# Two layers with a 3x3 convolution and a pole-residue spectral layer: a new border between forward transform and mixing, and the exponentials' argument reduction done by halves

## The chip, the cores and the metric

The kernel runs on one core of a Trainium2 chip, in one launch. The metric is the device time of that core in microseconds (us); lower is better. A core has TensorE (PE, whose weight loads are listed as PEld), VectorE (DVE), ScalarE (ACT), GpSimd (POOL) and SyncE (SP, which here only issues DMAs). Each engine works through its own queue in order.

## The reference

All data are float32; `x` has 16 images (B) of 16 channels (C) and 256x256 points (N).

```python
x = x + conv3x3_circular(groupnorm(x))            # layer 0
x = x + spectral(groupnorm(x))                    # layer 1

def spectral(x):
    alpha  = fft2(x)
    A, Bm  = 1/(omega1 - pole1), 1/(omega2 - pole2)       # 4 poles each per channel pair
    S      = einsum('ikpq,oikp,xikq->oxik', residue, A, Bm)
    r1     = einsum('biox,oxik->bkox', alpha, S)          # mixes the channels at each frequency
    r2     = einsum(alpha, A, Bm, residue)                # 'bkpq'
    x1     = ifft2(r1).real
    E1, E2 = exp(pole1 * ty), exp(pole2 * tx)             # complex exponentials
    x2     = einsum(r2, E1, E2).real
    return x1 + x2 / Nx / Ny
```

## The kernel before, in words

P is 128, the number of partitions. The program has four stages one after the other:

1. **Convolution** (to about 565 us): layer 0, with tables for later stages made beside it.
2. **Forward transform** (to about 1194 us): 64 units, four per channel, each one channel and four images. A unit loads rows, folds them (DVE, POOL), transforms lines (PE into `ps_y`, ACT L793 out) and columns (PE into `ps_x` and `psd`, ACT L833 copies `q`, DVE L837 to L840 writes the spectrum `spec`). After the fourth unit of a channel, `project` multiplies `psd` by a table (DVE L865, tile `pr`) and adds it up (POOL L866, `proj`), and `spec` goes to DRAM as `aD`, on SP's queue, for the last channel on ACT's (L976).
3. **Mixing** (about 1219 to 1861 us): 32 groups `g` of four rows of frequencies, each in four steps `n`.
4. **Inverse transform** (to the end), which also takes in the exponentials from DRAM (`eD`).

In the mixing the order on every engine is the order in which the program is written (a hand order, without a scheduler). For each group there is:

- `weights(g)`: DVE L903 to L919, eight operations of 128x128, make the products `v` of A, and one POOL operation (L930) spreads them into `w`. For group 0 four ACT copies (L927) do that in the place of POOL. It is a generator, advanced one part at a time between other work. In the loop, weights of group g+2 are made in group g.
- `sums(n, w)`: 32 matmuls (L1032) that give a quarter of S for one group, into `ps_s`. `spread` copies them to the tile `sg` with ACT (L1049) and DVE stream shuffles (L1052). Group g+1's sums stand beside group g's mixing.
- `mix`: 64 matmuls per step (L1120) from `sg` and the loaded spectrum `abd` into four banks `ps_mix`, then four evictions to `yt` (L1233; three by ACT and one by DVE, or two and two when the step before has said `late`), then the store of `yt` to `yD` (SP, L1134) and the load of the next group's `abd` (SP, L1102 and L1107).
- one step of `exps`, a generator (`make_exps`) of the exponentials E1 and then E2, from group 1 on. It has 16 parts q (eight for each, two channels i per part) with seven steps each. Written as the engines see it: **first step** POOL makes the argument `th` (two of 128x256, L1180) and `rn`, the number of whole turns (L1181, L1183, L1184); **second** POOL subtracts `rn` times c1 and c2 from `th` (L1190 multiplies into `tmp`, L1191 subtracts); **third** the same with c3, two clamps (L1194, L1195), and ACT's two Exp of 128x256 into `ex` (L1198), which says `late`; fourth nothing; **fifth** ACT's Sin of `th` (L1201), `late` too; sixth POOL multiplies and folds into `ex` (L1203, L1205); seventh SP stores `ex` to `eD` (L1210; two stores per q for E1, one for E2). `th`, `rn`, `tmp` and `ex` have one buffer each; all but the two arguments of Exp are 128x512. In the profile `ex` is `s_ex`, `th` is `s_th`, `rn` is `s_rn`, `tmp` is `s_tmp`.

Frequencies come in pairs of a group and its mirror, so group 0 holds two halves: rows of group 0 proper (first 128 columns) and those of "group 32". **The border** before the loop is `first_sums`: POOL clears `pair` (`abd` 0 and 1, L1058), weights of 0 are finished and those of 32 made at once (L1059), the first `abd` loads are issued, `accs` is added on DVE (L1062), and then for both halves and four n the sums are made and copied: 128 columns to `sg` and two values to a small tile `other`, with group 1's weights made in between. DVE corrects two special columns with `other` (L1078, L1079), POOL clears `abd` 2 and 3 (L1081), and their loads follow. `finish_projections` (L1090 to L1092) turns `accs` with the table `jmat` into `o2`, for x2.

Memory: the tiles' pools are laid out by hand; a pool that reuses the place of another waits for that tile's last user.

Of the kernel before, what the change touches and what calls it, by code (L numbers as in the profile page):

```python
# [16 lines left out]
B = 16  # L17
# [7 lines left out]
def conv_then_laplace_kernel(ctx: ExitStack, tc: tile.TileContext, a: dict, out: bass.AP):  # L25
# [33 lines left out]
    cols = const("cols", [P, 24])  # L59
    kmask = const("kmask", [P, C])  # L60
    fold2 = const("fold2", [P, 2, 64])
    o2 = cp.tile([P, B, 2, 16], FP, name="o2", tag="o2")
    proj = cp.tile([P, 2, B, 16, 2], FP, name="proj", tag="proj")
    jmat = cp.tile([P, 3, P], FP, name="jmat", tag="jmat")

    def pitched(name, rows, row, *split):

# [87 lines left out]
    own = m16[:, 0:C:2]  # L155
    load_consts()
    halves[1] = [load_x(1, h) for h in range(2)]
    nc.sync.dma_start(out=jmat, in_=a["jmat"])
    ones = tp.tile([P, P], FP, name="ones", tag="ones")
    nc.vector.memset(ones, 1.0)  # L160
    tiny = wp.tile([P, 8], FP, name="tiny", tag="tiny")
# [567 lines left out]
    kpp = pool(p1, "sines", 3)  # L729
    prp = pool(p1, "prod", 2)  # L730
    bp = pool(p1, "b_const")
    u0 = pool(p1, "u0")
    pa = pool(p1, "p_y", 3, space=PSUM)
    px = pool(p1, "p_x", 4, space=PSUM)
    pd = pool(p1, "p_d", space=PSUM)
# [134 lines left out]
    units = [(i, b0) for i in range(C) for b0 in range(0, B, 4)]  # L870
    p2 = ExitStack()
    kp = pool(p2, "m_const", side="right")
    up = {"v": pool(p2, "v", side="right"), "u0": u0}

    p2k = kp.tile([P, 32, 2], FP, name="p2k", tag="p2k")
    nc.sync.dma_start(out=p2k, in_=a["pole2_k"])
# [18 lines left out]
    def weights(g):  # L895

        shape = [P, 32, 4]
        u = up["u" if g else "u0"].tile([P, 4, 32, 4], FP, name="u", tag="u")  # L900
        w, den, e, f = (u[:, j] for j in range(4))
        pr2, pre, pim = (prU[:, j].unsqueeze(2).to_broadcast(shape) for j in range(3))
        nc.vector.tensor_tensor(  # L903
            w,
            omg[:, g].unsqueeze(1).to_broadcast(shape),
            pims.unsqueeze(2).to_broadcast(shape),
            ALU.subtract,
        )
        nc.vector.tensor_tensor(den, w, w, ALU.mult)
        nc.vector.tensor_tensor(den, den, pr2, ALU.add)  # L910
        yield
        nc.vector.reciprocal(den, den)

        nc.vector.scalar_tensor_tensor(e, w, m1, pre, ALU.mult, ALU.add)
        nc.vector.scalar_tensor_tensor(f, w, nm0, pim, ALU.mult, ALU.add)
        yield
        v = up["v"].tile([P, 32, 2, 4], FP, name="v", tag="v")
        nc.vector.tensor_tensor(v[:, :, 0], e, den, ALU.mult)
        nc.vector.tensor_tensor(v[:, :, 1], f, den, ALU.mult)  # L919
        if g == 0:  # L920
            yield
        wt = wp.tile([P, 4, 8, 32], FP, name="w", tag="w")
        v2 = v.rearrange("p a r s -> p a (r s)")
        w4 = wt.rearrange("p a k (i m) -> p (a k) i m", i=4)
        if g == 0:
            for i in range(4):
                nc.scalar.activation(w4[:, :, i], v2, AF.Copy, scale=m4[:, i : i + 1])  # L927
            return wt
        full = [P, 32, 4, 8]
        nc.gpsimd.tensor_tensor(  # L930
            w4,
            v2.unsqueeze(2).to_broadcast(full),
            m4.unsqueeze(1).unsqueeze(3).to_broadcast(full),
            ALU.mult,
        )
        return wt
# [3 lines left out]
    nc.vector.memset(sgn[:, 0:1], -1.0)  # L940
    nc.vector.memset(sgn[:, 1:2], 1.0)
    rest = v_stats(B - 4, B, lambda: pa.tile([P, 512], FP, name="ps_y", tag="ps_y"))
    last, first_weights = None, weights(0)
    for u in range(len(units) + 1):
        at = units[u] if u < len(units) else None
        if at is not None:
            now = vq
            t = lp.tile([P, 2, 4, 3, P], FP, name="t", tag="t")
            if u + 1 < len(units):
                vq = fold(*units[u + 1], loaded.pop(u + 1))  # L950
                if u + 3 < len(units):
                    loaded[u + 3] = load_v(*units[u + 3])
                if u < 2:
                    next(rest)
            for j in range(2):
                lines(*at, now, t, j)
        if last is not None:
            i, b0 = last[:2]
            if b0 == 0:
                spec = (a0, a1)[i % 2].tile([P, 2, N, B], FP, name="spec", tag="spec")  # L960
                psd = pd.tile([P, B, 32], FP, name="psd", tag="psd")
            done = columns(*last, spec, psd)
        if at is not None:
            for j in range(2, 4):
                lines(*at, now, t, j)
                if u < 2:
                    next(rest, None)
        if u == len(units) - 4:
            first_constants()
        if len(units) - 4 < u < len(units):  # L970
            next(first_weights)
        if last is not None:
            first_slots(b0, spec, *done)
            if b0 == B - 4:
                project(i, psd)
                (nc.sync if i + 1 < C else nc.scalar).dma_start(  # L976
                    out=aD[:, 2 * i : 2 * i + 2], in_=spec.rearrange("p r f b -> p r (f b)")
                )
        last = (*at, t) if at is not None else None
    p1.close()  # L980
    ptab.close()
# [14 lines left out]
    pm = pool(p2, "p_mix", 4, space=PSUM)  # L996

    def new_sg(g):
        return (g0, g1)[g % 2].tile([P, N, 2 * C], FP, name="sg", tag="sg")

# [4 lines left out]
        z.tile([P, 4, 4, 16, B], FP, name=f"abd{j}", tag=f"abd{j}") for j, z in ((2, a1), (3, a2))  # L1005
    ]

    zp.tile([P, 384], FP, name="between", tag="between")
    ct = tp.tile([P, 4, 8, N], FP, name="ct", tag="ct")
    nc.sync.dma_start(out=ct, in_=cD)  # L1010
    def next_step(steps, w):
# [10 lines left out]
            except StopIteration as e:  # L1022
                return e.value

    def sums(n, w):

        ps = [pg.tile([P, 2, N], FP, name="ps_s", tag="ps_s") for _ in range(2)]
        for q in range(2):
            for iq in range(4):
                for odd in range(2):  # L1030
                    rows = slice(64 * odd, 64 * odd + 64)
                    nc.tensor.matmul(  # L1032
                        ps[odd][32 * iq : 32 * iq + 32, q],
                        lhsT=w[rows, iq, 2 * n + q],
                        rhs=ct[rows, iq, 2 * n + q],
                        start=True,
                        stop=True,
                    )
        return ps
# [14 lines left out]
    def first_sums():  # L1054
# [1 line left out]


        nc.gpsimd.memset(pair, 0.0)  # L1058
        wt, w128 = at_once(first_weights), at_once(weights(32))  # L1059
        load(0, 1)  # L1060
        steps, w1 = weights(1), None
        nc.vector.tensor_tensor(accs, proj[:, :, :, :, 0], proj[:, :, :, :, 1], ALU.add)  # L1062
        sg = new_sg(0)
        other = up["u"].tile([P, 2, 2 * C], FP, name="other", tag="other")
        for h, w in enumerate((wt, w128)):
            for n in range(4):
                fy = slice(P * h, P * h + P)
                ps = sums(n, w)
                spread(
                    n,  # L1070
                    (sg[:, fy], [z[:, :, fy].rearrange("p q n -> p n q") for z in ps]),
                    (other[:, 1 - h], [z[:, :, P * (1 - h)] for z in ps]),
                )
                if 4 * h + n in (3, 4, 5):
                    w1 = next_step(steps, w1)
        for h in range(2):
            o, d = sg[:, P * h], other[:, h]
            nc.vector.tensor_tensor(d, d, o, ALU.subtract)  # L1078
# [1 line left out]
        for jq in range(2, 4):  # L1080
            nc.gpsimd.memset(abd[jq], 0.0)  # L1081
            load(0, jq)
        return sg, w1

    def finish_projections():


        for ro in range(2):
            ps = pm.tile([P, B, 16], FP, name="ps_o", tag="ps_mix")
            nc.tensor.matmul(ps, lhsT=jmat[:, 0], rhs=accs[:, ro], start=True, stop=False)  # L1090
            nc.tensor.matmul(ps, lhsT=jmat[:, 2 - ro], rhs=accs[:, 1 - ro], start=False, stop=True)
            nc.vector.tensor_copy(o2[:, :, ro], ps)  # L1092

    def load(g, jq, rows=range(4)):

# [65 lines left out]
    def make_exps(which):  # L1161
# [10 lines left out]
        nc.gpsimd.tensor_scalar(pim, pl[:, :, 1], sign, None, ALU.mult)  # L1172
        for q in range(8):
            th = ep.tile([P, 2, N], FP, name="s_th", tag="s_th")
            rn = ep.tile([P, 2, N], FP, name="s_rn", tag="s_rn")
            tmp = ep.tile([P, 2, N], FP, name="s_tmp", tag="s_tmp")
            ex = ep.tile([P, 2, N], FP, name="s_ex", tag="s_ex")
            for j in range(2):
                i = 2 * q + j
                nc.gpsimd.tensor_scalar(th[:, j], t, pim[:, i : i + 1], None, ALU.mult)  # L1180
            nc.gpsimd.tensor_scalar(rn, th, 1.0 / (2 * PI), turns, ALU.mult, ALU.add)  # L1181
            magic = 1.5 * 2.0**23
            nc.gpsimd.tensor_scalar(rn, rn, magic, None, ALU.add)  # L1183
            nc.gpsimd.tensor_scalar(rn, rn, magic, None, ALU.subtract)  # L1184
            yield
            c1 = 6.28125
            c2 = float(np.float32(1.93500518798828125e-3))
            c3 = 2 * np.pi - c1 - c2
            for c in (c1, c2, c3):
                nc.gpsimd.tensor_scalar(tmp, rn, float(c), None, ALU.mult)  # L1190
                nc.gpsimd.tensor_tensor(th, th, tmp, ALU.subtract)  # L1191
                if c == c2:
                    yield
# [21 lines left out]

    p2.enter_context(tc.manual_schedule())
    accs = yp.tile([P, 2, B, 16], FP, name="accs", tag="yt")
    ahead, wt = first_sums()
    finish_projections()
    unmix = None  # L1220
    exps, late = chain(make_exps(0), make_exps(1)), None
    for g in range(32):
# [1 line left out]
        steps = weights(g + 2) if g < 30 else iter(())  # L1224
        ahead = new_sg(g + 1) if g < 31 else None
        for n in range(4):
            evict = sums(n, w_now) if ahead is not None else []
            yt = yp.tile([P, 2, 4 * B, 16], FP, name="yt", tag="yt")
            if evict:
                spread(n, (ahead, [z.rearrange("p q n -> p n q") for z in evict]))  # L1230
            for m in range(4):
                o, src = mix(4 * n + m, sg, yt)
                (nc.vector.tensor_copy if m >= (2 if late else 3) else nc.scalar.copy)(o, src)  # L1233
# [376 lines left out]
```

## Time and profile before

| what | us |
|---|---|
| median of three runs | 2618.05 (2610.47 to 2623.62) |
| profiled execution | 2623.94 |
| its span | 2622.1, mean granted TensorE clock 0.986 |
| mixing, 1219 to 1861 | 642, PE busy 602.5, DVE 504.9, ACT 406.9, POOL 389.2 |

A timeline row gives the start and the length in us, the engine, the line and operation, the tiles written and read, the shapes, how many there were, and in square brackets how long the engine had been idle before and what ended that. A row may stand for several instructions one after the other ("x64"); matmuls are pipelined and their lengths overlap. A row of a group gives the count, then busy us and mean ns, then the idle time ahead. A row of one line gives least, median and largest ns of one. A granted clock of 0.50 means that PE ran at half speed.

### The profile page before, as it was taken

To read this page: it belongs to the slowest core of one execution; us is meant where nothing else is said; L and a number is where in the kernel's file an instruction comes from. 1 tells how busy PE (TensorE), PEld (TensorE's weight loads), DVE (VectorE), ACT (ScalarE), POOL (GpSimd) and SP (SyncE) were. 2 spreads that over 40 slices of the span, in tenths; PEclk is the share of its full clock that TensorE was granted. 3 is DMA by queue.
4 is the path that set the end of the run, shared out by engine and by line. 5 is a ranking of instruction groups with operands and counts; after the bars stand their busy time and mean duration, and the time that the engine had idled before them with its cause. 6 is when DMAs were issued, how large, how long until landed. Compare 5 with 4: busy or idle time off the path is not lost.

```text
span 2622.1 us, 84262 instructions
## 1 busy us (share of the span) xinstructions
PE 2468.6 (94%) x35314; PEld 1885.3 (72%) x35314; DVE 1980.8 (76%) x3772; ACT 1432.6 (55%) x2599; POOL 1290.5 (49%) x1179
## 2 busy tenths in 40 slices
PE   5998999989999999998999999999799999999998
PEld 2444455567777777775878778788688888888887
DVE  7777788848888888887877878887276676667666
ACT  2565566666666666665666656666244444444443
POOL 1333378433333333333666645766555565555553
PEclk9999999989999999999999999999899999999999
DMA  7888878854655655655777777777988888888884
GB/s 274 276 279 282 294 270 294 297 211 177 240 195 209 242 220 194 245 225 190 225 229 214 226 225 222 222 227 228 253 302 289 291 292 279 299 289 287 291 287 174
DMA packets 318011, 653.17 MB, mean 249 GB/s; under 512 B 49174, under 2 KB 163990, under 8 KB 305728
## 3 DMA queue, kind: packets, MB, share of 16 engines
q1 hardware_dynamic: 316464, 640.57, 72.4%
q8 instruction: 278, 4.55, 0.7%
q0 software_dynamic: 896, 3.02, 0.4%
q10 hardware_dynamic: 272, 4.19, 0.4%
q14 instruction: 101, 0.83, 0.1%
HBM read 368.15 MB, written 280.36 MB: 247 GB/s over the span
## 4 chain that ended last, share of the span: by engine, by line
PE 58%; DVE 7%; DMA 4%; SPq 3%; ACT 3%; POOL 2%; issue 1%; ACTq 0%; DVEq 0%; POOLq 0%
PE ps_mix L1120 9%; PE ps_y L777 9%; PE ps_y L785 8%; PE ps_p L1361 7%; PE ps_f L1385 7%; PE ps_f L1386 7%; PE ps_x L820 5%; DMA yD<-yt 4%; PE ps_s L1032 2%; SPq L1134 2%; PE ps_h L1345 2%; PE psd L805 1%; DVE r L1394 1%; DVE ol L1396 1%; DVE ol L1397 1%
## 5 line engine op out<-in xcount | busy, mean ns | idle before, releaser
L1120 PE MATMUL ps_mix<-abd,sg 128*64 128x128 f32 x8192 | 482.2, 276 | 39.4 <-DMA yD<-yt 16.6
L1120 PEld LDWEIGHTS ps_mix<-abd,sg 128*64 128x64 f32 x8192 | 451.9, 138 | 92.9 <-ACT yt L1233 55.7
L1325 POOL TENSOR_TENSOR u<-yk 128x512 f32<-128x512 f32 (+1 forms) x268 | 358.2, 1369 | 314.7 <-PE ps_p L1361 249.1
L305 PE MATMUL ps_conv<-xt,wc 32*32 32x512 f32 x12288 | 445.6, 602 | 36.0 <-issue 26.1
L305 PEld LDWEIGHTS ps_conv<-xt,wc 32*32 32x32 f32 x12288 | 251.1, 103 | 217.6 <-issue 127.0
L793 ACT ACTIVATE t<-ps_y,vmr 128x384 f32<-128x384 f32 x512 | 297.1, 580 | 161.1 <-PE ps_y L785 161.1
L1052 DVE STREAM_SHUFFLE sg<-ps_s 128x512 f32<-128x512 f32 (+1 forms) x264 | 329.1, 1316 | 0.0
L777 PE MATMUL ps_y<-tabE,vq 128*128 128x256 f32 x1024 | 313.2, 388 | 11.0 <-DVE vq L766 9.4
L785 PE MATMUL ps_y<-tabO,vq 128*128 128x256 f32 x1024 | 305.9, 380 | 0.0
L275 POOL TENSOR_TENSOR pair<-pair,far 128x1024 f32<-128x1024 f32 x64 | 151.7, 2370 | 304.1 <-DVE pair L272 207.7
L1385 PE MATMUL ps_f<-pt,inv 128*128 128x256 f32 x1008 | 300.4, 380 | 0.0
L1386 PE MATMUL ps_f<-hs,ey 128*128 128x256 f32 x1008 | 299.8, 379 | 0.0
L1361 PEld LDWEIGHTS ps_p<-inv,u 128*128 128x128 f32 x2048 | 268.9, 193 | 35.4 <-POOL u L1329 10.9
L1389 DVE TENSOR_TENSOR r<-ps_f,q 128x256 f32<-128x256 f32 x256 | 107.0, 418 | 241.9 <-ACT q L1388 241.9
L1361 PE MATMUL ps_p<-inv,u 128*128 128x128 f32 x2048 | 276.2, 278 | 9.8 <-POOL u L1329 9.7
L1049 ACT ACTIVATE sg<-ps_s,mcol 128x512 f32<-128x512 f32 (+1 forms) x264 | 179.3, 689 | 192.2 <-DVE sg L1052 117.1
L777 PEld LDWEIGHTS ps_y<-tabE,vq 128*128 128x128 f32 x1024 | 189.6, 191 | 87.5 <-ACT q L833 51.2
L1388 ACT COPY q<-ps_f 128x256 f32<-128x256 f32 x256 | 95.4, 373 | 274.7 <-PE ps_f L1386 250.4
L1363 ACT COPY pt<-ps_p 128x512 f32<-128x512 f32 x256 | 151.5, 592 | 134.9 <-PE ps_p L1361 134.9
L765 POOL TENSOR_TENSOR vq<-vf 128x512 f32<-128x512 f32 x64 | 81.4, 1272 | 291.6 <-DVE vf L769 281.5
L785 PEld LDWEIGHTS ps_y<-tabO,vq 128*128 128x128 f32 x1024 | 195.4, 191 | 26.9
L1233 ACT COPY yt<-ps_mix 128x512 f32<-128x512 f32 x352 | 184.1, 592 | 55.8 <-DMA yD<-yt 42.2
(237 smaller groups left out, 3993.6 us busy)
## 6 DMA issues: line engine op xcount, KB each, us to landing
xt<-in_x SPq DMA_DIRECT2D x288, 258.0 KB
vD<-pair SPq DMA_DIRECT2D x256, 256.0 KB
yD<-yt SPq DMA_DIRECT2D x512, 128.0 KB
vl<-vD SPq DMA_DIRECT2D x128, 512.0 KB
out_y<-ol SPq DMA_DIRECT2D x128, 512.0 KB
s<-vD SPq DMA_DIRECT2D x126, 512.0 KB
aD<-spec SPq DMA_DIRECT2D x15, 4096.0 KB
yk<-yD SPq DMA_DIRECT2D x60, 1024.0 KB
```

The costliest lines, as they stand in the source:

```text
L305: nc.tensor.matmul(acc[r][32 * c : 32 * c + 32], lhsT=ready[b][0][rows, phase, tap], rhs=halves[b][u // 2][rows, q : q + 5 : 4, 2 - tap : ...
L777: nc.tensor.matmul(ps[:, 0:N], lhsT=vf[:, xo, 0, j], rhs=tabE[:, 0 : i + 2 : i + 1], start=True, stop=False, skip_group_check=True,)
L785: nc.tensor.matmul(ps[:, P : P + N], lhsT=vf[:, xo, 1, j], rhs=tabO[:, i : C + 1 : C - i], start=False, stop=True, skip_group_check=True,)
L793: nc.scalar.activation(t[:, xo, j].rearrange("p l n -> p (l n)"), ps[:, 0:384], AF.Copy, scale=vmr[:, 0, b0 + j, i : i + 1],)
L1049: nc.scalar.activation(to[..., k : k + 2], src[odd], AF.Copy, scale=nsgn)
L1052: nc.vector.stream_shuffle(to[..., C + k : C + k + 2], src[1 - odd], swap)
L1120: nc.tensor.matmul(ps[64 * t : 64 * t + 64, j], lhsT=sg[:, f : f + 2].rearrange("p f m -> p (f m)"), rhs=abd[jq][:, :, 2 * t + cc, 2 * jj ...
L1233: (nc.vector.tensor_copy if m >= (2 if late else 3) else nc.scalar.copy)(o, src)
L1325: nc.gpsimd.tensor_tensor(u[:, :, j].rearrange("p b (c n) -> p c b n", c=8), in0, in1, o)
L1361: nc.tensor.matmul(ps[:, at], lhsT=u[:, n], rhs=tab, start=True, stop=True)
L1385: nc.tensor.matmul(ps[:, e], lhsT=tab, rhs=pt[:, e], start=True, stop=False)
L1386: nc.tensor.matmul(ps[:, e], lhsT=ey[:, e], rhs=hs, start=False, stop=True)
```

## The change

- **Weights of group 32** are made in the forward stage as group 0's are: constants at unit 57 and not 60, group 0's three parts at units 58 to 60, group 32's at 61 to 63. Both go to `w` by ACT's four copies, and `u0` and `v` get a second buffer.
- **Special columns**: `sg` of even groups has room for 257 columns. For group 32 the sums are made with the two halves of the columns reversed (`turned`), so that the special column comes with the others: one eviction of 129 columns instead of 128 and two values. `other` is copied from `sg` by ACT.
- **Group 1's weights and sums** move into the mixing of group 0: weights at once ahead of n=0, and sums of no set, set 0, set 1, sets 2 and 3 at n = 0, 1, 2, 3.
- `accs` is added on POOL; `jmat` is loaded into the place of `s_ex`, on SP's queue ahead of the first `abd` load (it was loaded at the start of the kernel); `o2` is put in `proj`'s place; the last `aD` store is issued in two pieces, rows 0 to 15 and 16 to 127.
- **Exponentials**: `rn` is 128x256, `tmp` has no tile of its own but is the half `ex[:, j]`, and the reduction is done for one half j at a time: first step `th` and the nine operations of j=0, second step the nine of j=1 (all of 128x256), third step the clamps and Exp. There are seven steps as before.

```diff
-    o2 = cp.tile([P, B, 2, 16], FP, name="o2", tag="o2")
-    jmat = cp.tile([P, 3, P], FP, name="jmat", tag="jmat")
...
-    u0 = pool(p1, "u0")
+    u0 = pool(p1, "u0", 2)
...
-        if g == 0:
+        if g % 32 == 0:
             for i in range(4):
                 nc.scalar.activation(w4[:, :, i], v2, AF.Copy, scale=m4[:, i : i + 1])
...
-    last, first_weights = None, weights(0)
+    last, first_weights = None, [weights(0), weights(32)]
...
-        if u == len(units) - 4:
+        if u == len(units) - 7:
             first_constants()
-        if len(units) - 4 < u < len(units):
-            next(first_weights)
+        if len(units) - 7 < u < len(units):
+            next(first_weights[(u - len(units)) // 3 + 2])
...
-                (nc.sync if i + 1 < C else nc.scalar).dma_start(
-                    out=aD[:, 2 * i : 2 * i + 2], in_=spec.rearrange("p r f b -> p r (f b)")
-                )
+                for rows in (slice(0, P),) if i + 1 < C else (slice(0, 16), slice(16, P)):
+                    (nc.sync if i + 1 < C else nc.scalar).dma_start(
+                        out=aD[rows, 2 * i : 2 * i + 2],
+                        in_=spec[rows].rearrange("p r f b -> p r (f b)"),
+                    )
...
-        wt, w128 = at_once(first_weights), at_once(weights(32))
+        wt, w128 = (at_once(steps) for steps in first_weights)
         load(0, 1)
-        steps, w1 = weights(1), None
-        nc.vector.tensor_tensor(accs, proj[:, :, :, :, 0], proj[:, :, :, :, 1], ALU.add)
+        nc.gpsimd.tensor_tensor(accs, proj[:, :, :, :, 0], proj[:, :, :, :, 1], ALU.add)
...
-                fy = slice(P * h, P * h + P)
-                ps = sums(n, w)
+                ps = sums(n, w, h == 1)
+                fy = slice(P * h, P * h + P + 1)
                 spread(
-                    n,
-                    (sg[:, fy], [z[:, :, fy].rearrange("p q n -> p n q") for z in ps]),
-                    (other[:, 1 - h], [z[:, :, P * (1 - h)] for z in ps]),
+                    n, (sg[:, fy], [z[:, :, 0 : P + 1].rearrange("p q n -> p n q") for z in ps])
                 )
-                if 4 * h + n in (3, 4, 5):
-                    w1 = next_step(steps, w1)
+            nc.scalar.copy(other[:, 1 - h], sg[:, P * (1 + h)])
...
+    jmat = ep.tile([P, 3, P], FP, name="jmat", tag="s_ex")
+    nc.sync.dma_start(out=jmat, in_=a["jmat"])
...
-            rn = ep.tile([P, 2, N], FP, name="s_rn", tag="s_rn")
-            tmp = ep.tile([P, 2, N], FP, name="s_tmp", tag="s_tmp")
+            rn = ep.tile([P, N], FP, name="s_rn", tag="s_rn")
...
-            nc.gpsimd.tensor_scalar(rn, th, 1.0 / (2 * PI), turns, ALU.mult, ALU.add)
...
-            for c in (c1, c2, c3):
-                nc.gpsimd.tensor_scalar(tmp, rn, float(c), None, ALU.mult)
-                nc.gpsimd.tensor_tensor(th, th, tmp, ALU.subtract)
-                if c == c2:
-                    yield
+            for j in range(2):
+                z, tmp = th[:, j], ex[:, j]
+                nc.gpsimd.tensor_scalar(rn, z, 1.0 / (2 * PI), turns, ALU.mult, ALU.add)
+                nc.gpsimd.tensor_scalar(rn, rn, magic, None, ALU.add)
+                nc.gpsimd.tensor_scalar(rn, rn, magic, None, ALU.subtract)
+                for c in (c1, c2, c3):
+                    nc.gpsimd.tensor_scalar(tmp, rn, float(c), None, ALU.mult)
+                    nc.gpsimd.tensor_tensor(z, z, tmp, ALU.subtract)
+                yield
...
-            evict = sums(n, w_now) if ahead is not None else []
+            if g == 0 and n == 0:
+                w_now = at_once(weights(1))
+            sets = () if ahead is None else (n,) if g else ((), (0,), (1,), (2, 3))[n]
+            evict = [(j, sums(j, w_now)) for j in sets]
```

More of the change, by code (lines that the diff above doesn't have):

```diff
@@ L157, in conv_then_laplace_kernel @@
     halves[1] = [load_x(1, h) for h in range(2)]
-    nc.sync.dma_start(out=jmat, in_=a["jmat"])
     ones = tp.tile([P, P], FP, name="ones", tag="ones")
@@ L872, in conv_then_laplace_kernel @@
     kp = pool(p2, "m_const", side="right")
-    up = {"v": pool(p2, "v", side="right"), "u0": u0}
+    up = {"v": pool(p2, "v", 2, side="right"), "u0": u0}
     p2k = kp.tile([P, 32, 2], FP, name="p2k", tag="p2k")
@@ L899, in weights @@
         shape = [P, 32, 4]
-        u = up["u" if g else "u0"].tile([P, 4, 32, 4], FP, name="u", tag="u")
+        u = up["u" if g % 32 else "u0"].tile([P, 4, 32, 4], FP, name="u", tag="u")
         w, den, e, f = (u[:, j] for j in range(4))
@@ L924, in weights @@
         w4 = wt.rearrange("p a k (i m) -> p (a k) i m", i=4)
-        if g == 0:
+        if g % 32 == 0:
             for i in range(4):
@@ L998, in new_sg @@
     def new_sg(g):
-        return (g0, g1)[g % 2].tile([P, N, 2 * C], FP, name="sg", tag="sg")
+        return (g0, g1)[g % 2].tile([P, N + 1 - g % 2, 2 * C], FP, name="sg", tag="sg")[:, 0 : N + (g == 0)]
     pair = a0.tile([P, 4, 4, 2, 16, B], FP, name="abd01", tag="abd01")
@@ L1006, in conv_then_laplace_kernel @@
     ]
-    zp.tile([P, 384], FP, name="between", tag="between")
+    zp.tile([P, 1088], FP, name="between", tag="between")
     ct = tp.tile([P, 4, 8, N], FP, name="ct", tag="ct")
@@ L1023, in at_once, with sums @@
                 return e.value
-    def sums(n, w):
+    def sums(n, w, turned=False):
         ps = [pg.tile([P, 2, N], FP, name="ps_s", tag="ps_s") for _ in range(2)]
@@ L1031, in sums @@
                     rows = slice(64 * odd, 64 * odd + 64)
+                    c = ct[rows, iq, 2 * n + q].rearrange("p (h n) -> p h n", h=2)
                     nc.tensor.matmul(
-                        ps[odd][32 * iq : 32 * iq + 32, q],
+                        ps[odd][32 * iq : 32 * iq + 32, q].rearrange("p (h n) -> p h n", h=2),
                         lhsT=w[rows, iq, 2 * n + q],
-                        rhs=ct[rows, iq, 2 * n + q],
+                        rhs=c[:, ::-1] if turned else c,
                         start=True,
@@ L1082, in first_sums @@
             load(0, jq)
-        return sg, w1
+        return sg
+    jmat = ep.tile([P, 3, P], FP, name="jmat", tag="s_ex")
+    nc.sync.dma_start(out=jmat, in_=a["jmat"])
     def finish_projections():
+        o2 = cp.tile([P, B, 2, 16], FP, name="o2", tag="proj")
         for ro in range(2):
@@ L1092, in finish_projections @@
             nc.vector.tensor_copy(o2[:, :, ro], ps)
+        return o2
     def load(g, jq, rows=range(4)):
@@ L1180, in make_exps @@
                 nc.gpsimd.tensor_scalar(th[:, j], t, pim[:, i : i + 1], None, ALU.mult)
-            nc.gpsimd.tensor_scalar(rn, th, 1.0 / (2 * PI), turns, ALU.mult, ALU.add)
             magic = 1.5 * 2.0**23
-            nc.gpsimd.tensor_scalar(rn, rn, magic, None, ALU.add)
-            nc.gpsimd.tensor_scalar(rn, rn, magic, None, ALU.subtract)
-            yield
             c1 = 6.28125
@@ L1188, in make_exps @@
             c3 = 2 * np.pi - c1 - c2
-            for c in (c1, c2, c3):
-                nc.gpsimd.tensor_scalar(tmp, rn, float(c), None, ALU.mult)
-                nc.gpsimd.tensor_tensor(th, th, tmp, ALU.subtract)
-                if c == c2:
-                    yield
+            for j in range(2):
[7 more added lines that the diff above has]
+                yield
             nc.gpsimd.tensor_scalar(th, th, phase, 3.1415925, ALU.add, ALU.min)
@@ L1217, in conv_then_laplace_kernel @@
     accs = yp.tile([P, 2, B, 16], FP, name="accs", tag="yt")
-    ahead, wt = first_sums()
-    finish_projections()
+    ahead, wt = first_sums(), None
+    o2 = finish_projections()
     unmix = None
@@ L1226, in conv_then_laplace_kernel @@
         for n in range(4):
-            evict = sums(n, w_now) if ahead is not None else []
+            if g == 0 and n == 0:
+                w_now = at_once(weights(1))
+            sets = () if ahead is None else (n,) if g else ((), (0,), (1,), (2, 3))[n]
+            evict = [(j, sums(j, w_now)) for j in sets]
             yt = yp.tile([P, 2, 4 * B, 16], FP, name="yt", tag="yt")
-            if evict:
-                spread(n, (ahead, [z.rearrange("p q n -> p n q") for z in evict]))
+            for j, ps in evict:
+                spread(j, (ahead, [z.rearrange("p q n -> p n q") for z in ps]))
             for m in range(4):
```

## The prediction

> **What bounds the kernel now.** I read the page first, then the timeline at the border between the forward transform and the mixing, then the waits and timelines inside the mixing (1219 to 1861 us), where most of the edit runs.
>
> The page, busy time and costliest groups:
>
> ```profile
> PE 2468.6 (94%) x35314; PEld 1885.3 (72%) x35314; DVE 1980.8 (76%) x3772; ACT 1432.6 (55%) x2599; POOL 1290.5 (49%) x1179
> L1120 PE MATMUL ps_mix<-abd,sg 128*64 128x128 f32 x8192 | 482.2, 276 | 39.4 <-DMA yD<-yt 16.6
> ```
>
> TensorE bounds it, in the mixing too: 602.5 of its 642 us there are busy. What can be won is its idle time; what can be lost is any wait that holds it. The border, PE then DVE:
>
> ```profile
> 1204.59 6.72 PE L1032 MATMUL ps_s<-ct,w 64*32 64x256 f32 x128 [9.01 <-ACT other L1049]
> 1219.12 4.00 PE L1120 MATMUL ps_mix<-abd,sg 128*64 128x128 f32 x64
> 1239.19 2.08 PE L1120 MATMUL ps_mix<-abd,sg 128*64 128x128 f32 x34 [1.04 <-DMA yD<-yt]
> ...
> 1198.11 0.98 DVE L903 TENSOR_TENSOR u<-kgrp,pims 128x128 f32<-128x128 f32 x1
> 1202.21 0.28 DVE L919 TENSOR_TENSOR v<-u 128x128 f32<-128x128 f32 x1
> 1203.03 0.72 DVE L1052 STREAM_SHUFFLE sg<-ps_s 128x256 f32<-128x256 f32 x1
> ```
>
> PE waits 9 us while DVE makes the weights of group 32 ahead of its first shuffle; mixing starts at 1219.1, group 1's at 1239.2. In the mixing, POOL and ACT around step q=2 of the exponentials (POOL's argument reduction; ACT's Exp):
>
> ```profile
> 1333.12 1.84 POOL L1180 TENSOR_SCALAR s_th<-s_t,s_pim 128x256 f32<-128x256 f32 x2
> 1341.16 0.91 ACT L1198 ACTIVATE s_ex<-s_t,s_pl 128x256 f32<-128x256 f32 x2
> 1345.37 3.47 PEld L1120 LDWEIGHTS ps_mix<-abd,sg 128*64 128x64 f32 x64 [0.41 <-ACT yt L1233]
> 1346.47 1.28 POOL L1191 TENSOR_TENSOR s_th<-s_th,s_tmp 128x512 f32<-128x512 f32 x1
> 1351.69 1.89 POOL L930 TENSOR_TENSOR w<-v,mcol 128x1024 f32<-128x1024 f32 x1
> ```
>
> Exp runs while POOL is still reducing (to 1347.75): nothing ties them. Right behind the Exp stand ACT's evictions, which PE waits for. What an ACT hold costs PE, in the one place where it has a like one:
>
> ```profile
> 1376.83 1.56 ACT L1233 COPY yt<-ps_mix 128x512 f32<-128x512 f32 x3 [3.97 <-DMA yD<-yt]
> 1378.35 6.64 PE L1120 MATMUL ps_mix<-abd,sg 128*64 128x128 f32 x64 [3.17 <-DMA yD<-yt]
> ```
>
> A hold of 3.97 us idles PE 3.17, and the next 64 matmuls take 6.64 instead of 3.71; the granted clock is 0.94 in 1360 to 1380 and 0.89 in 1380 to 1400.
>
> **Part by part.** The sum is against the profiled execution: 2,623.9 us, span 2,622.1; the median of the runs is 2,618.05, 5.9 lower.
>
> *Weights of group 32 in the forward stage.* In its last three units PE keeps 9.57 us per unit with a weight step in each, so three more hide behind PE: 0. ACT gets four more copies (L927's four took 1.69 us) beside 44% idle: the last `q` copies slip perhaps 0.5. Cover gone, this is at most 1.7.
>
> *Border.* From DVE's queue go 4.3 us of weights (1198.11 to 1202.49), `accs` (0.68; to POOL, behind its projections, which end 1200.2, so PE's `ps_o` has it in time), 16 `other` shuffles (0.25 each, overlapping) and group 1's weights (2.9). Eight sets at 1.3 to 1.45 us from 1198.7 end at about 1209 to 1210; the fix (0.8) lets mixing start near 1211, 8 us earlier. Group 1's weights then stand beside the first mixing step: DVE 2.9 plus POOL 1.9 is 4.8 against 3.7 of mixing, with DVE's two `o2` copies (0.75) ahead, so PE waits about 2; four sum sets at 1.02 and four mixes at 3.7 follow. Group 1's mixing starts near 1234 instead of 1239.2: **−5**. Bounds: −2 (the sums keep today's rhythm) and −10 (PE's 9.0 idle all goes, with little coming back). On SP `jmat` goes ahead of the first load; today that load starts at 1209.2, after the last `aD` store, so one issue (0.4 to 0.6 for such rows) is covered; POOL's two memsets (6.97, today from 1217.2) come ahead of group 1's `w`, the second not before that store is out, so they end near 1213 and the loads behind them (6.0 of SP) start sooner; the split store costs a second issue on ACT's queue (0.39) and lets the load begin earlier: 0. Reversed sums read the same number of columns: 0. Only in this part can there be a gain.
>
> *Exponentials: price.* Nine POOL operations of 128x512 become eighteen of 128x256. Rows:
>
> ```profile
> L1190 POOL TENSOR_SCALAR s_tmp<-s_rn 128x512 f32<-128x512 f32 x48 | 71.6, 1491 | 4.1
> L1191 POOL TENSOR_TENSOR s_th<-s_th,s_tmp 128x512 f32<-128x512 f32 x48 | 61.5, 1281 | 4.0
> L1181 POOL TENSOR_SCALAR s_rn<-s_th,cols 128x512 f32<-128x512 f32 x16 | 11.1, 693 | 1.7
> L584 POOL TENSOR_SCALAR s_cden<-s_space x16: 912/923/1882, 345.9 to 459.3; 128x256 f32<-128x256 f32 x16
> L585 POOL TENSOR_TENSOR s_cden<-s_cden x16: 612/612/1217, 347.0 to 461.3; 128x256 f32<-128x256 f32 x16
> L587 POOL TENSOR_SCALAR s_parts<-s_space,s_nm x16: 542/548/1576, 349.6 to 462.9; 128x256 f32<-128x256 f32 x16
> ```
>
> One half: 0.55 + 2×0.92 + 3×(0.92+0.61) + nine gaps of 0.09 = 7.8 us (6.8 if every 512 row simply halves, 8.1 with L1205's 0.73 for the subtraction). I take 7.8, rows of the same width and operation. The first yield now holds `th` (1.9) and one half, 9.7; the second 7.8.
>
> *Exponentials: new waits.* `tmp` is now Exp's own output tile, so Exp of half j waits until POOL has finished half j. And POOL's first write to `tmp`, 4.6 us into the step (th 1.94, rn 2.66), waits until the last `eD` store has read that tile, about 2.6 us after its issue ends (the last one's issue ended 1844.56, POOL went on at 1847.44). Queued behind Exp on ACT are sum evictions and `yt` evictions, which free PE's banks; queued behind POOL's reduction is `w` (L930), the next group's weights, for which PE waits. I walked all sixteen q's through their rows:
>
> - q = 1, 5, 9, 13. Example q=1: POOL starts 1293.88, `tmp` is due at 1298.5, but the store's issue ends 1298.47, so it lands about 1301.1; the second half ends 1293.9 + 17.5 + 2.6 = 1314.0, where Exp's second half stood ready at 1308.0: ACT holds 6.0. The four: 6.0, 7.7, 6.8, 6.0, mean 6.6.
> - q = 2, 6, 10, 14. Example q=2: 1333.12 + 17.5 = 1350.6 against 1341.6: 9.0. The four average 8.2.
> - From a hold PE is covered 0.8 in the row above; with the banks and yields around the Exp I take 1.3: 4×5.3 + 4×6.9 = **49**.
> - q = 3, 7, 11, 15: the store is issued late (q=3: ends 1368.43), POOL waits for it with `w` behind, which starts at 1371.0 today: first half done 1376.2, `w` 1378.1, PE needs it at 1374.1. The four are late by 4.0, 3.5, 2.6, 0.9: 11; Exp's hold comes on top, 5.7 less up to 4.0 that the late step absorbs, about 3 each: **23** (11 to 29).
> - q = 4, 12: both halves stand ahead of `w`, 7.1 and 7.5 late: **15**. q = 0, 8: no earlier store, reduction done when `w` is due: 0.
>
> That is 87. Of PE's present waits on `yD` in the mixing (16.6 in 12) nearly all vanish under these: −15 (bounds 0 and −17). Cold clock: 14 stalls of 3 to 8 us; the row above paid 2.9 after 3.2. I take 1.7 each, **+24**, just over the midpoint of 0 and 2.9 (0 where PE waits for ACT's backlog anyway).
>
> The Trainium skill (TensorE: Matmul & The Clock Gate, HAM oscillation) says that no gap of PE may exceed about 3.4 us, or the clock halves until some 3.4 us of work have passed. The row above fell cold after 3.17, near it; by the rule each stall would cost about 1.7 at half speed, the same 24, and a border wait kept below 3.4 would spare PE its stretch at 0.50 (1200 to 1210).
>
> Sum: 87 − 15 + 24 − 5 = **+91** on 2,623.9, so 2,715 as profiled and **2,708** against the median. Low: prices halved −27 (14 × 1.9), no cold clock −24: +40, 2,658. High: +10 for price, +17 for 2.9 cold each, no absorption +15: +133, 2,751.
>
> **Rivals.**
> 1. *Not slower: PE rides over ACT's hold.* The mixing step has four banks of sums mixed ahead, and ACT sits idle for 235 of the 642 us, so it could catch up and nothing of the 87 be seen. Then only the border counts: −5, 2,613, at the bound of −10 2,608. Decisive is the cover: holds average 7.4, so PE needs over 7 us of it. Against it, the row above shows 0.8, and PE waits for ACT's `yt` 55.7 us already.
> 2. *Only `w` is late.* If Exp's wait mostly falls where ACT is held by `yD` anyway (42.2 us in all), POOL's growth of 2.8 per q (2×7.8 against 12.8) in the eight groups where `w` starts just behind a reduction leaves 8×2 − 5 = +11, 2,629. Against: 1341.16 was not such a place.
> 3. *It feeds on itself.* A q has 7 steps of 4.67, 32.7 us; POOL needs 9.7+7.8+3.5, 2.8 for the products and some 3.3 for `w`, 27.1, plus the store wait. A late Sin delays the store, which delays the next q. A further 2 to 3 us per q: +40, 2,750.
>
> **How the numbers follow.** The runs before spread over 13 us, 0.5%, about what a measurement can tell from no change. Forecast (2,658 to 2,751) 0.65; above it (rival 3) 0.10; a milder loss between rival 2 and it 0.07; rival 1 0.12, split over faster (border at its −10 and more, under 2,605) 0.06 and same 0.06; rival 2 0.06, half of it same. Faster 0.06, same 0.09, slower 0.85. The range, 2,622 to 2,760, leaves out rival 1 and the top of rival 3, together under 2 in 10.
>
> **What would show it.** Right: ACT's Exp (L1198) with idle of 6 to 9 us behind POOL's subtraction; POOL's first multiply into `s_ex` behind `eD<-s_ex`; PE behind `yt` or `w` by several us in 14 places, with cold clock after; the mixing near 735 us instead of 642; border 5 us shorter. Wrong: Exp waits of 1 us, 256-wide operations at 0.7 or less, or the mixing at 642.

## The result, and the profile after

The changed kernel took 2713.76 us (median of six runs, 2709.28 to 2721.12) against 2619.66 for the kernel before in its six runs: ratio 1.0363, 95% interval 1.0345 to 1.0380. That is 94 us slower. The profile after spans 2713.2 us at a mean granted clock of 0.968. Lines from the border on have moved a little: `mix` is L1121 (L1120 before), POOL's `w` L927 (L930), the `yt` evictions L1236 (L1233), POOL's multiply into `tmp` L1191 (L1190) and its subtraction L1192 (L1191).

The page after, busy time and the costliest group, as they were shown of before:

```profile
PE 2500.4 (92%) x35314; PEld 1918.0 (71%) x35314; DVE 1968.7 (73%) x3739; ACT 1432.9 (53%) x2589; POOL 1327.9 (49%) x1323
L1121 PE MATMUL ps_mix<-abd,sg 128*64 128x128 f32 x8192 | 511.6, 287 | 87.5 <-ACT yt L1236 75.8
```

The same 8192 matmuls of the mixing have 87.5 us of idle time ahead of them instead of 39.4, nearly all behind ACT's evictions, and are themselves 29.4 us longer. The waits of the mixing after (engine, line, what ended the wait: us in all, times, longest) name the engine behind ACT:

```profile
ACT s_ex L1198 <- POOL s_th L1192: 108.8, 22, 7.5
PE ps_mix L1121 <- ACT yt L1236: 75.8, 13, 7.8
POOL s_ex L1191 <- DMA eD<-s_ex: 58.5, 10, 9.0
PE ps_s L1032 <- POOL w L927: 25.5, 6, 8.9
PE ps_mix L1121 <- DMA yD<-yt: 3.8, 2, 3.2
```

The first and third did not exist before; the fourth was 0.9 us (on the weight loads), the fifth 16.6. The timeline of the changed kernel at q=1, POOL, ACT and PE:

```profile
1299.87 0.85 POOL L1191 TENSOR_SCALAR s_ex<-s_rn 128x256 f32<-128x256 f32 x1 [5.60 <-DMA eD<-s_ex]
1312.02 0.72 POOL L1192 TENSOR_TENSOR s_th<-s_th,s_ex 128x256 f32<-128x256 f32 x1
...
1305.08 0.51 ACT L1198 ACTIVATE s_ex<-s_t,s_pl 128x256 f32<-128x256 f32 x1 [1.04 <-POOL s_th L1192]
1312.78 0.51 ACT L1198 ACTIVATE s_ex<-s_t,s_pl 128x256 f32<-128x256 f32 x1 [7.20 <-POOL s_th L1192]
1314.33 1.07 ACT L1236 COPY yt<-ps_mix 128x512 f32<-128x512 f32 x2
...
1314.97 5.16 PE L1121 MATMUL ps_mix<-abd,sg 128*64 128x128 f32 x64 [7.81 <-ACT yt L1236]
```

Read it downwards: POOL waits 5.6 us until the `eD` store has left `s_ex`; each Exp starts right after POOL's last subtraction of its half; ACT is held 1.04 + 7.20 us, its next evictions of `ps_mix` start at 1314.33, and PE is idle for 7.81, after which its 64 matmuls take 5.16 instead of 3.71. The granted clock was 0.61 from 1310 to 1315 and 0.75 from 1315 to 1321.

The border after (PE, POOL and SP):

```profile
1194.85 4.76 PE L1032 MATMUL ps_s<-ct,w 64*32 64x256 f32 x96 [4.09 <-ACT sg L1049]
1213.55 6.39 PE L1121 MATMUL ps_mix<-abd,sg 128*64 128x128 f32 x64 [7.29 <-DMA abd<-aD]
1235.76 3.71 PE L1121 MATMUL ps_mix<-abd,sg 128*64 128x128 f32 x64
...
1211.18 3.51 POOL L1077 MEMSET abd<- 128x4096 f32 x1 [11.22 <-DMA aD<-spec]
...
1199.60 7.94 SPq L1103 DMA_DIRECT2D abd<-aD  x4
```

The convolution and the forward stage ended 5.2 us earlier in this execution (first border sums at 1188.42, before at 1193.62), so times are counted from the first sums. PE's 9.0 us of idle time are 4.1, and DVE's corrections end 18.6 us after them (25.7 before). But mixing starts only at 25.1 (25.5 before): PE now waits 7.29 us for the first `abd` load. Group 1's mixing, third row, starts at 47.3 (45.6 before). The border has become 1.8 us longer.

### The profile page after: what moved, and what is told of

It reads as the page before. It is cut to its first block, busy times and chain, and to the rows that moved or that the text cites. A ratio compares the mean times of both kernels' runs of the same rounds, so it can differ in the third digit from the quotient of the medians.

```text
span 2713.2 us, 84361 instructions
## 1 busy us (share of the span) xinstructions
PE 2500.4 (92%) x35314; PEld 1918.0 (71%) x35314; DVE 1968.7 (73%) x3739; ACT 1432.9 (53%) x2589; POOL 1327.9 (49%) x1323
## 4 chain that ended last, share of the span: by engine, by line
PE 59%; POOL 7%; DVE 5%; DMA 3%; SPq 2%; ACT 2%; issue 1%; ACTq 0%; DVEq 0%; POOLq 0%
PE ps_mix L1121 11%; PE ps_y L774 9%; PE ps_y L782 8%; PE ps_p L1364 7%; PE ps_f L1388 7%; PE ps_f L1389 7%; PE ps_x L817 4%; PE ps_s L1032 2%; POOL s_ex L1191 2%; POOL s_th L1192 2%; PE ps_h L1348 2%; PE psd L802 1%; SPq L1135 1%; DVE r L1397 1%; DMA yD<-yt 1%
## 5 line engine op out<-in xcount | busy, mean ns | idle before, releaser
L1121 PE MATMUL ps_mix<-abd,sg 128*64 128x128 f32 x8192 | 511.6, 287 | 87.5 <-ACT yt L1236 75.8
L1121 PEld LDWEIGHTS ps_mix<-abd,sg 128*64 128x64 f32 x8192 | 481.0, 145 | 141.8 <-ACT yt L1236 96.4
L1236 ACT COPY yt<-ps_mix 128x512 f32<-128x512 f32 x352 | 184.7, 592 | 48.0 <-DMA yD<-yt 25.8
```

Source lines behind the costliest of these rows:

```text
L1121: nc.tensor.matmul(ps[64 * t : 64 * t + 64, j], lhsT=sg[:, f : f + 2].rearrange("p f m -> p (f m)"), rhs=abd[jq][:, :, 2 * t + cc, 2 * jj ...
```

## The experiments

The theory from the prediction (**A**): ACT's Exp stands behind POOL's halves because `tmp` shares its tile, POOL's first half stands behind the `eD` store for the same reason, and `w` stands behind both. Its rivals: the border (**B**), POOL's longer work as such (**C**), parts of the exponentials that feed on each other (**D**), a store's wait that is only a symptom (**G**). In every run the filler tile `between` is resized by what the tiles of the exponentials gained or lost, so the places behind it stay; the cuts below leave that line out.

**The exponentials' part alone** on the kernel before:

```diff
-            rn = ep.tile([P, 2, N], FP, name="s_rn", tag="s_rn")
-            tmp = ep.tile([P, 2, N], FP, name="s_tmp", tag="s_tmp")
+            rn = ep.tile([P, N], FP, name="s_rn", tag="s_rn")
...
+            for j in range(2):
+                z, tmp = th[:, j], ex[:, j]
...
```

> The kernel before with the exponentials' part of the change alone (rn of one half, tmp in ex, halves one after the other); the border is that of before. Theory A (ACT's Exp behind POOL's halves, POOL's first half behind the eD store, w behind both): nearly the whole loss is here, +93 to +99 us, ratio 1.036 to 1.038, and PE's idle behind yt and w is near the 101 us of the changed kernel. Rival B (the loss comes from the border, whose new order sends loads and sums into the mixing late): ratio 1.00 to 1.01.

Measured: 1.0363 (1.0330 to 1.0397). Its waits repeat those of the changed kernel:

```profile
ACT s_ex L1197 <- POOL s_th L1191: 110.6, 22, 8.4
PE ps_mix L1120 <- ACT yt L1232: 78.9, 13, 8.4
PE ps_s L1032 <- POOL w L930: 25.1, 6, 8.8
```

The whole loss is in this part; rival B falls.

**The border alone**, the reverse of that diff on the changed kernel:

> The changed kernel with the exponentials' part undone (rn and tmp whole, in tiles of their own). Theory A: the border is worth about 2 us, since group 1's mixing starts 47.3 us after the first sums in the profile of before and 45.6 in that of the changed kernel: ratio 0.998 to 1.000. Rival B: 1.03.

Measured: 1.0012 (0.9995 to 1.0030). The expectation has its two numbers the wrong way round: it is 45.6 us in the profile of before and 47.3 in the changed one, so theory and traces should have said 2 us slower. That fits the measurement, whose interval still holds no change.

**An own tile for `tmp`**, still by halves:

```diff
+            tmp = ep.tile([P, N], FP, name="s_tmp", tag="s_tmp")
...
-                z, tmp = th[:, j], ex[:, j]
+                z = th[:, j]
```

> The changed kernel with tmp in a tile of its own of 128x256; the reduction still goes by halves. Theory A: Exp and the first half lose their waits; what stays is POOL's price, which puts w late: in the eight groups where it stands just behind the clamps by 2 to 2.5 us, in q = 0, 4, 8, 12 by about 2.4: +20 us over before (bounds +8 to +35), ratio 1.003 to 1.013. Rival C (it is POOL's longer work as such that costs, not who waits for it): as the changed kernel, 1.03 to 1.04.

Measured: 1.0046 (1.0031 to 1.0061), about +12 us. One tile of 1 KB per partition takes back most of the loss, and rival C falls: POOL does the same 1323 instructions as in the changed kernel (1319.1 us busy against 1327.9). What stays is mostly `w`; the longest wait behind `yt` is at the end of the mixing, where the kernel before has one of 8.2. The waits of this run:

```profile
PE ps_s L1032 <- POOL w L927: 23.1, 10, 2.9
PE ps_mix L1121 <- ACT yt L1237: 9.9, 5, 7.1
```

**Exp a step later**, everything shared as in the change:

```diff
-            for j in range(2):
-                i = 2 * q + j
-                nc.scalar.activation(ex[:, j], t, AF.Exp, scale=pl[:, i, 0:1])
-            yield True
-            yield
+            yield
+            for j in range(2):
+                i = 2 * q + j
+                nc.scalar.activation(ex[:, j], t, AF.Exp, scale=pl[:, i, 0:1])
+            yield True
```

> The changed kernel with ACT's two Exp in the fourth step and not the third, all tiles shared as in the change. Theory A: a step is 4.67 us, so holds that average 7.4 shrink to 2.7 and PE, which rides over 1.3, loses 8 times 1.4; w's lateness (25.5 us in the changed kernel) stays with its cold clock: +45 us over before (30 to 60), ratio 1.012 to 1.023. Rival D (the parts feed on each other, POOL is the bound of the mixing): the hold only moves to the Sin or the next part, ratio 1.03 or more.

Measured: 1.0201 (1.0173 to 1.0228), +53. ACT's holds fall from 108.8 us to 33.0:

```profile
PE ps_s L1032 <- POOL w L927: 46.0, 10, 8.7
ACT s_ex L1199 <- POOL s_th L1192: 33.0, 13, 3.6
```

But PE's wait for `w`, which the expectation left at 25.5, is 46.0. The trace shows where: at q = 1, 5, 9, 13 PE now stands 7.4, 7.3, 6.0 and 4.8 us behind `w` (25.4 together), where in the changed kernel it stood 25.2 behind ACT, and `w` starts 23 to 26 us after its part's first POOL operation, as before (23 to 27). So `w` was late enough there for the whole stall, and Exp's hold had hidden it.

**Two buffers of `ex`**: the store's wait goes, Exp's stays:

```diff
-            ex = ep.tile([P, 2, N], FP, name="s_ex", tag="s_ex")
+            ex = ep.tile([P, 2, N], FP, name="s_ex", tag="s_ex" if q % 2 else "s_ey")
```

> The changed kernel with two buffers of ex in turn, so that POOL's first half no longer waits for the eD store (58.5 us of POOL in 10 places); Exp still waits for POOL's halves. Theory A, by its rows: q = 1, 5, 9, 13 hold ACT about 4 us instead of 6.6, the 2, 6, 10, 14 stay (8.2), 3, 7, 11, 15 lose their late w and nearly all of their hold, 4 and 12 have w late by 2.4 instead of 7.3: 44 us of PE in place of 87, and 14 instead of 24 of cold clock: +50 over before (35 to 65), ratio 1.013 to 1.025. Rival G (the eD wait is only a symptom of the held ACT): 1.03 or more.

Measured: 1.0187 (1.0166 to 1.0208), +48. PE hardly waits for `w` any more, and ACT is held 64.5 us instead of 108.8:

```profile
ACT s_ex L1198 <- POOL s_th L1192: 64.5, 18, 7.2
PE ps_s L1032 <- POOL w L927: 6.2, 2, 3.4
```

The store's wait is a cause of its own, for `w` and for part of the holds; rival G falls.

**Both of these together:**

> The changed kernel with both remedies, two buffers of ex and Exp in the fourth step; tmp still shares ex and the reduction goes by halves. Each alone left +48 and +53 over before. Theory A: with the store's wait gone and Exp a step later, holds of about 7 shrink to 2 to 2.5, of which PE rides over 1.3, and w is late as in the run with an own tmp (23 us in ten places, 13 more than what it replaces): +12 to +25, ratio 1.005 to 1.010. If the two waits only trade places (POOL too slow for the mixing, the parts feeding on each other), +35 or more, 1.013.

Measured: 1.0069 (1.0045 to 1.0092), +18. The two remedies take 94 us down to 48 and 53 alone and to 18 together (46 and 41 won alone, 76 together), so each of the two waits costs by itself. The sum of the single gains exceeds the joint one by 11 us, which is about what the intervals of the four measurements leave open.

**Sharing without halves:** `tmp` is `ex`, and the reduction is whole.

```diff
-            tmp = ep.tile([P, 2, N], FP, name="s_tmp", tag="s_tmp")
+            tmp = ex
```

> The border alone with tmp sharing ex's tile, but the reduction whole as before, in 512-wide operations (the sharing without the halves). Theory A: both waits are there, but smaller, since tmp is first written 5.9 us into a part and last read 14.6 us into it (4.6 and 17.5 with halves): holds of about 2.6 (q = 1, 5, 9, 13), 6.5 (2, 6, 10, 14) and 2 (3, 7, 11, 15), w on time but in 4 and 12: 31 us of PE, part of it in place of yD waits, 10 of cold clock, +3 for the border: +38 over before (20 to 55), ratio 1.008 to 1.021. If the halves were the cause, 1.000 to 1.004; if the sharing by itself were the whole cause, 1.03 or more.

Measured: 1.0265 (1.0243 to 1.0287), +69, above the range. Sharing alone makes nearly three quarters of the loss. I had counted holds at twelve of the sixteen parts, most of them shorter; the profile has all sixteen, 2.5 to 7.4 us each, 76.5 in all. It also shows POOL waiting 46.7 us in nine places for ACT's Sin (18.3 before):

```profile
ACT s_ex L1199 <- POOL s_th L1192: 76.5, 16, 7.4
POOL s_th L1204 <- ACT s_th L1202: 46.7, 9, 7.2
```

A held ACT is late with the Sin, and POOL then late with the next part. That would be a small form of rival D, but no run separates it from a plain slip of the parts against the steps. Where the estimate was short shows in the profile, which is 60 us longer than that of before. Outside the border's first step the matmuls of the mixing are 24 us longer, where I had taken 10 of cold clock; PE's idle there rose by some 33, where 31, part of it in place of `yD` waits, was expected.

**The border in one store** (the border alone, with the last `aD` store whole, as before):

```diff
-                for rows in (slice(0, P),) if i + 1 < C else (slice(0, 16), slice(16, P)):
...
+                (nc.sync if i + 1 < C else nc.scalar).dma_start(
+                    out=aD[:, 2 * i : 2 * i + 2], in_=spec.rearrange("p r f b -> p r (f b)")
+                )
```

> The border alone, with the last store of aD in one piece as before. In the border-alone run PE waited 6.9 us for the first abd load, whose four issues took 7.6 us beside the rest of that store. Theory E (the load competes with the store's second piece): in one piece the load starts 15 us after the first sums and not 11, but goes through in 2.6 us and lands about 20 to 22 us after them, 3 to 5 earlier than now: 3 us faster than the border alone, ratio 0.998 to 1.000. Theory F (the load is slow whatever runs beside it): it starts 4 us later and lands 4 later, ratio 1.002 to 1.004.

Measured: 0.9993 (0.9979 to 1.0007); this interval overlaps that of the border alone, so what follows is read from one trace of each. SP and PE:

```profile
1209.77 2.58 SPq L1101 DMA_DIRECT2D abd<-aD  x4
1216.13 6.55 PE L1119 MATMUL ps_mix<-abd,sg 128*64 128x128 f32 x64 [5.45 <-DMA abd<-aD]
```

First sums were at 1192.48. The load starts 17.3 us after them, 6.1 later than in the run with the border alone (11.2), and goes through in 2.6 us instead of 7.6; mixing starts at 23.7 instead of 25.7, group 1's at 46.0 instead of 48.1. So beside the store's second piece the load lost more than the early start gave.

**The rest of the store behind the load:**

```diff
+        nc.sync.dma_start(
+            out=aD[16:P, 2 * C - 2 : 2 * C], in_=spec[16:P].rearrange("p r f b -> p r (f b)")
+        )
```

(after `load(0, 1)`; ACT's queue issues rows 0 to 15 alone)

> The border alone, with rows 16 to 127 of the last store issued on SP's queue behind the first abd loads. Theory E: the first loads have the DMA engines for themselves, PE's 6.9 us behind abd go and mixing starts about 19 us after the first sums instead of 25.7; the store's rest lands later, so the clearing of abd3 and its load may hold the fourth step by up to 3: ratio 0.996 to 0.999. Theory F: no change against the border alone, 1.000 to 1.002.

Measured: 1.0008 (0.9994 to 1.0023), a miss: 0.996 to 0.999 was expected. Mixing starts 18.1 us after the first sums, as theory E says, but its second step waits longer than was won (PE, then POOL):

```profile
1210.72 4.16 PE L1124 MATMUL ps_mix<-abd,sg 128*64 128x128 f32 x64 [0.45 <-DVE sg L1078]
1227.00 1.96 PE L1032 MATMUL ps_s<-ct,w 64*32 64x256 f32 x32 [12.12 <-POOL w L927]
...
1221.58 3.51 POOL L1080 MEMSET abd<- 128x4096 f32 x1 [17.37 <-DMA aD<-spec]
1225.06 1.89 POOL L927 TENSOR_TENSOR w<-v,mcol 128x1024 f32<-128x1024 f32 x1
```

POOL's clearing of `abd3` waits for the store, and group 1's `w` stands behind it.

**Group 1's weights back ahead of the mixing** (one store, weights(1) and its sums where they were):

> The border alone with one store, and group 1's weights and its first sums back ahead of the mixing as in the kernel before. In the one-store run mixing began 23.7 us after the first sums, PE having waited 5.4 for the abd load, and its first 64 matmuls took 6.55 at a lowered clock; group 1's mixing began at 46.0 (45.6 in the kernel before). Theory E (the store and load of aD set the start, so DVE has 5 us to spare ahead of it and the move of group 1's weights bought nothing): mixing still begins at about 23.7, with its sums beside every step, and group 1's begins at 43 to 44: 2 to 3 us faster than the one-store run, ratio 0.997 to 1.000. Rival H (DVE sets the start): mixing begins 3 later and nothing is won, 1.000.

Measured: 1.0012 (0.9993 to 1.0031). In the trace mixing starts 24.3 us after the first sums and group 1's 44.5, 1.5 earlier than in the one-store run and 1.0 earlier than in the kernel before; the time, for which up to 1.000 was expected, does not show it.

**That, with the store's rest behind the load and `abd3` later** (cleared and loaded after the first step's store):

> As the run with group 1's weights back, with rows 16 to 127 of the last store behind the first loads on SP, and the clearing and load of abd3 behind the first step's store. Theory E: the first load no longer counts and mixing begins when DVE is done, about 21 to 22 us after the first sums (18.1 where the store was put behind the loads, plus the 2.9 of group 1's weights); abd3 arrives about 39 after them, some 3 to 5 late for the fourth step: group 1's mixing at 42 to 45, ratio 0.996 to 1.000. If instead the loads of abd3 hold SP's queue and the yt stores with it, 1.001 to 1.003.

Measured: 1.0025 (1.0007 to 1.0043), a miss: theory E had 0.996 to 1.000. Mixing starts at 20.0, then ACT's first copy of group 1's sums waits 8.59 us, PE 5.19 behind ACT, and group 1's mixing starts at 46.2. The profile puts ACT's wait down to an `abd` load; but ACT goes on at 1227.59, and POOL's clearing of `abd3`, which waits for the store's rest, at 1227.48, so it may be the store again. Each of these borders moved the wait and none shortened the whole by an amount that a run can tell; I found no version faster than the kernel before.

## Why the prediction was right

The forecast was 2,708 (2,618.05 + 91 is 2,709); the median is 2,714. By the steps of the sum:

- **POOL's price.** Half of a part was to take 7.8 us. At q=1 the second half runs from 1305.16 to 1312.74: 7.6. The rows are 0.85 (0.92 assumed), 0.73 (0.61) and 0.48 (0.55). Right.
- **Exp's holds.** PE was to lose 49 at q = 1, 5, 9, 13 and 2, 6, 10, 14, and the stalls behind `yt` there are 25 and 31. At q=1 ACT is held 8.2, not 6.0: the store landed 4.3 us after its issue ended and not 2.6 (the row that 2.6 was taken from gives 2.9). Over these eight the holds average 8.3 instead of 7.4, and PE rides over 0.4 to 1.7 of them, 1.3 on average, as assumed. For q = 3, 7, 11, 15 the forecast was 23; they cost 13 behind `yt` and 9 behind `w`. For 4 and 12, 15; 16 behind `w`. ACT's holds add up to more (108.8 against some 71 in my walk), as at q = 4, 12 I counted none and they have 15.9, and at q = 3, 7, 11, 15 they have 26.6 and not 12; but for much of that time PE already stood behind `w`.
- **Cover and absorption.** Those stalls make 94, where I had 87. PE's idle in the mixing rose by only 66 (from 39.4 to 80.2 ahead of mixes, without the border's 7.3, and from 0 to 25.5 ahead of sums), so 28 of today's idle was absorbed, not 15: waits behind `yD` (16.6 to 3.8), and also ones behind ACT's `sg` and short ones behind `yt`, which I had not named. Net 66 against 72.
- **Cold clock.** +24 was taken. The matmuls of the mixing grew by 29.4 and the sums by 3.8, of which the border's first mix has 2.4: +31. The term was mis-sized, in count and in price: 18 stalls of 2.5 to 8.9 us, not 14, each paid about 2.1 us (37 in all), less 6.6 that three stalls of the kernel before had paid and that the sum had not taken off. The prediction priced one row, as the only one of its kind; the profile of before has two more (64 matmuls in 5.38 us after 3.27 of idle, 5.68 after 8.20), and the three average 2.2.
- **The border: this step failed.** I had −5; the traces give +1.8, the border alone 1.0012. What failed is "the split store ... lets the load begin earlier: 0". The load did begin 4.4 us earlier, but took 7.9 us to issue beside the store's second piece, and PE waited for it 7.3 with a cold first step of 6.39. DVE's part of that step was right (done 18.6 us after the first sums; I had about 17).

From group 1's first mix to the last mix's end it is 621.2 us before and 718.1 after: +97, where the sum without the border was +96. That fit to 1 us owes something to misses that cancel: stalls +7, absorption −13, cold clock +7.

*Rival 1* (PE rides over the hold) had its deciding point at a cover of 7 us; at q=1 PE idles 7.81 behind a hold of 8.24. (The 55.7 us that it names as PE's wait for `yt` were those of the weight loads; PE's own were 13.8.) *Rival 2* is near what the run with an own `tmp` shows, by chance in the number: +12 with a border that won nothing, where I had +11 from 16 for `w` and −5 for the border. *Rival 3* did not happen to the point of 2,750, though POOL waits 40.5 us for the Sin now and 18.3 before.

## What to carry to other kernels

Two tiles that share a place share their waits: a scratch tile put into an output tile of another engine ties that engine, and the store that reads it, to every use of the scratch. Price it by walking each instance through the rows, asking how long the other engine's queue is held and how much its reader has in hand; here the reader, which bounds the kernel, had 0.4 to 1.7 us. And starting a load early by splitting the store it waits for gains nothing where the other piece runs beside the load, or where the next user in the queue waits for that piece.

## What the runs showed of the hardware

- A load's issues are slow beside a large store: four issues of the first `abd` load took 7.94 us beside the last `aD` store (7.57 in the run with the border alone), 2.57 to 2.58 after it.
- What a stall of PE costs in clock does not grow with its length: after 7.81 us of idle 64 matmuls took 5.16 instead of 3.71, after 7.62 it was 6.41, after 4.13 it was 6.44. It also comes after shorter ones than I had thought. Two rows of PE in the changed kernel, with 2.49 us of idle time between them (and 2.92 some 7 us earlier), and one of the kernel before:

```profile
1395.75 1.09 PE L1032 MATMUL ps_s<-ct,w 64*32 64x256 f32 x32
1399.34 5.38 PE L1121 MATMUL ps_mix<-abd,sg 128*64 128x128 f32 x64 [2.49 <-ACT yt L1236]
...
1798.23 3.71 PE L1120 MATMUL ps_mix<-abd,sg 128*64 128x128 f32 x64 [2.09 <-DMA abd<-aD]
```

The granted clock was 1.00 in 1396 to 1399.3 and 0.68 in 1399.3 to 1404.7. The Trainium skill (TensorE: Matmul & The Clock Gate, HAM oscillation) puts the bound at gaps over about 3.4 us. Here the measurement decides: 2.5 us of idle were enough in this place, while in the profile of before a gap of 2.09 left the next 64 at 3.71.

No shorter bound can be drawn either. Counted over all thirteen profiles of this case, wherever PE idled at least 0.5 us ahead of 64 mixing matmuls that stand in one row: of 139 gaps under 1.85 us none lengthened them, of 56 gaps of 1.85 to 3.5 us 34 did and 22 did not, and all 55 longer ones did, by 1.3 to 2.9 us. The extremes between are 1.85 us in the last border run (5.38 afterwards) and 3.46 in the run with group 1's weights back (3.71 afterwards, at a granted clock of 1.00).
